# A 4-bit FFN at the end of a decoder: quotients rounded in bf16 from their upper 16 bits, block elements at a pitch, block maxima by halving, and a written order

## The chip, the cores and the metric

The kernel runs on one core of one Trainium2 chip. The metric is device microseconds for one launch. TensorE (PE) does the matmuls and the transposes, VectorE (DVE) most elementwise work and the reductions, ScalarE (ACT) the activation functions and some copies, GpSimd (POOL) a few copies, a cross-partition maximum and some DMA issues; SyncE (SP) only issues DMAs.

## The reference, cut to what matters

A decoder of four layers, each with a self-attention, a cross-attention to a context of 375 rows and an FFN, on x of 8 batches x 112 tokens x 256. Every sublayer is `x = x + f(layernorm(x))`. The change touches the last FFN, whose three matrices and two activations are rounded to a 4-bit format in blocks of 16 consecutive elements:

```python
def fake_quant_nvfp4(x, global_scale):       # blocks of 16 along the last axis
    amax = max(abs(xb))                      # of each block
    sc8  = float8_e4m3fn(clip(amax / 6 * global_scale, 0, 448))
    dq   = sc8 / global_scale
    a    = clip(abs(xb) / dq, 0, 6)
    q    = sign(xb) * nearest of {0, .5, 1, 1.5, 2, 3, 4, 6}
    return q * dq

gate, up = q(x) @ q(gate_w).T, q(x) @ q(up_w).T          # 256 -> 1024
hidden   = silu(gate) * up
out      = q(hidden) @ q(down_w).T                       # 1024 -> 256
```

The weights' global scale is computed from the largest absolute weight of each matrix; the activations' scales are inputs.

## The kernel before

Tokens lie on partitions: 112 of them, one batch at a time, the eight batches side by side. `HB` is 4, half the batches; `HT` is 448, the tokens of a half. The twelve sublayers run one after the other. Within some of them the program's own scheduler orders the instructions of each engine; a `manual_schedule` block instead keeps, on the engines that it names, the order in which the Python code emits them. Each engine executes its list in order, so an instruction that waits holds up all behind it on that engine. Tiles are named by tag; a pool's `bufs` says how many copies of a tag exist, and a new use waits until the readers of the old one are done.

Three places matter here.

**The last FFN, `l3_ffn` (L1940).** It normalises all eight batches (`normalise`: `stats`, then one `tensor_scalar` for each batch, L435), quantises the result in two halves of 112 x 1024 elements, and transposes each half with PE (L1967) into `xqT`. Then, for four pairs of batches: for each batch and each half of the 1024 hidden columns, four matmuls fill the PSUM tile `gu` (two copies), ACT computes `sg`, the silu of the gate (L1983), and DVE the product `hid` (L1984). The pair's 2048 columns are quantised into `hq`, sixteen PE transposes (L1993) and two ACT copies make `hqT` (L1997), sixteen matmuls make the two tiles `y`, and two DVE instructions add them to x (L2001). There is no manual order in this FFN: the scheduler mixes the pairs.

**The helper `quantise` (L1848).** All on DVE. A block's elements are adjacent. It reduces a block to its largest magnitude (L1865), works out the block scale `qs` and the reciprocal `qz` in nine instructions on one element a block (L1867 to L1881), multiplies the source by `qz` (L1884), clamps to +-6 (L1885), isolates the exponent as int32 (L1887), makes from it a rounding constant (L1888), adds and subtracts it (L1889, L1890) and multiplies by the block scale into bf16 (L1891). Everything but the last output is fp32.

**The weights, `l3_weights` (L1893).** Each matrix is 128 x 2048. It is loaded by a POOL DMA into `raw` (one copy, so the next load waits until the last L1884 has read this one), reduced to block maxima `amax` (L1905) and to one column (L1909), POOL takes the maximum across partitions (`gs`, L1910), and two calls of `quantise` follow. This generator is advanced from `l2_ffn`, but the scheduler starts it earlier, between the instructions of the preceding MLP, `mha_mlp` of the second attention of layer 2: there, for each half, PE computes eight `mm` tiles (two copies), ACT takes their gelu `hT` (L1630), and after that PE fills a tile of 112 x 256 for each batch, which DVE adds to `xo` (L1638) and then to x (L1445). The statistics of x follow (L421, L422, then `va` L404 on DVE, the square root `sd` L405 on ACT, which needs a table load of its own, and small DVE steps).

The cross-attention ahead of the FFN (`l3_xattn`, the helper `cross`) has a manual order; the result of batch 3 is added to x (L474) in its middle, that of batch 7 at its end. The first layer's cross-attention `l1_xattn` uses the same helper in the same form.

Of the kernel before, what the change touches and what calls it, by code (L numbers as in the profile page):

```python
# [20 lines left out]
F32 = mybir.dt.float32  # L21
I32 = mybir.dt.int32
BF16 = mybir.dt.bfloat16
AF = mybir.ActivationFunctionType
ALU = mybir.AluOpType
AX = mybir.AxisListType
ET = mybir.EngineType
PSUM = bass.MemoryType.PSUM

P = 128  # L30
S, NB, D = 112, 8, 256
T = S * NB
HT = T // 2
HB = NB // 2
# [9 lines left out]
def _fm(w):  # L44

    k, n = w.shape
    return w.reshape(k // P, P, n).transpose(1, 0, 2).reshape(P, -1)
# [61 lines left out]
def _weights(inp):  # L109
# [3 lines left out]
    a, xa, f = g("L0_attn"), g("L0_xattn"), g("L0_ffn")  # L113
# [33 lines left out]
    a, xa, f = g("L1_attn"), g("L1_xattn"), g("L1_ffn")  # L147
# [23 lines left out]
    for j in range(3):  # L171
        cols = slice(512 * j, 512 * j + 512)
# [10 lines left out]
    a, xa, f = g("L2_attn"), g("L2_xattn"), g("L2_ffn")  # L183
# [44 lines left out]
    a, xa, f = g("L3_attn"), g("L3_xattn"), g("L3_ffn")  # L228
# [13 lines left out]
        ],  # L242
        [("l3x_wo", _fm(_spread(_slots(xa("Wo"))).T))],
    ]
    raw = [_fm(f("gate_w")), _fm(f("up_w")), _fm(f("down_w"))]
    v3 = [
        ("l3f_s_in", np.broadcast_to(f("s_in")[None, :], (P, 1))),
        ("l3f_s_in_down", np.broadcast_to(f("s_in_down")[None, :], (P, 1))),
# [99 lines left out]
class _Kernel:  # L348
# [1496 lines left out]
            )  # L1845
        w.done("l3x_wo")

    def quantise(self, pool, src, dst, rows, n, gs, amax=None):  # L1848


        nc = self.nc
        nb = n // 16

        def blocks(a):
            return a.rearrange("p (k e) -> p k e", e=16)

        def bc(a):
            return a[:, :, None].to_broadcast([rows, nb, 16])

        def sm(tag):  # L1860
            return self.t(pool, [P, nb], f"q{tag}{nb}")[:rows]

        if amax is None:
            amax = sm("m")
            nc.vector.tensor_reduce(amax, blocks(src), AX.X, ALU.max, apply_absolute_value=True)  # L1865
        sc, st, z = sm("s"), sm("t"), sm("z")
        nc.vector.tensor_scalar(sc, amax, 1.0 / 6.0, gs, ALU.mult, ALU.mult)  # L1867
        nc.vector.tensor_scalar(sc, sc, 448.0, None, ALU.min)


        big = 1.5 * 2.0**23
        nc.vector.tensor_scalar(
            st.bitcast(I32), sc.bitcast(I32), 0x7F800000, None, ALU.bitwise_and
        )
        nc.vector.tensor_scalar(st, st, 0.125 * big, 2.0**-9 * big, ALU.mult, ALU.max)
        nc.vector.tensor_tensor(sc, sc, st, ALU.add)
        nc.vector.tensor_tensor(sc, sc, st, ALU.subtract)
        nc.vector.scalar_tensor_tensor(z, sc, 0.0, sc, ALU.is_equal, ALU.add)
        nc.vector.reciprocal(z, z)

        nc.vector.tensor_scalar(z, z, gs, 1.0 + 2.0**-23, ALU.mult, ALU.mult)  # L1881
        a = self.t(pool, [P, n], f"qa{n}")[:rows]
        m = self.t(pool, [P, n], f"qm{n}")[:rows]
        nc.vector.tensor_tensor(blocks(a), blocks(src), bc(z), ALU.mult)  # L1884
        nc.vector.tensor_scalar(a, a, 6.0, -6.0, ALU.min, ALU.max)  # L1885

        nc.vector.tensor_scalar(m.bitcast(I32), a.bitcast(I32), 0x7F800000, None, ALU.bitwise_and)  # L1887
        nc.vector.tensor_scalar(m, m, 1.0, 0.5 * big, ALU.max, ALU.mult)  # L1888
        nc.vector.tensor_tensor(a, a, m, ALU.add)  # L1889
        nc.vector.tensor_tensor(a, a, m, ALU.subtract)  # L1890
        nc.vector.tensor_tensor(blocks(dst), blocks(a), bc(sc), ALU.mult)  # L1891

    def l3_weights(self, pool, ps):  # L1893


        nc = self.nc
        raws, wqs = {}, {}

        def loaded(i):
            raws[i] = self.t(pool, [P, COLS], "raw")  # L1900
            nc.gpsimd.dma_start(raws[i], self.args["in_wq"][i])

        def rounded(i, nk, no):
            amax = self.t(pool, [P, P], "amax")
            nc.vector.tensor_reduce(  # L1905
                amax, raws[i].rearrange("p (k e) -> p k e", e=16), AX.X, ALU.max, apply_absolute_value=True
            )
            top, gs = (self.t(pool, [P, 1], n) for n in ("top", "gs"))
            nc.vector.tensor_reduce(top, amax, AX.X, ALU.max)  # L1909
            nc.gpsimd.partition_all_reduce(gs, top, P, bass_isa.ReduceOp.max)  # L1910
            nc.vector.reciprocal(gs, gs)
            nc.vector.tensor_scalar(gs, gs, 448.0 * 6.0, None, ALU.mult)
            nc.vector.reciprocal(self.igs[:, i : i + 1], gs)
            wqs[i] = self.t(pool, [P, no, nk * P], "wq", BF16)
            flat = wqs[i].rearrange("p o k -> p (o k)")
            for h in range(2):
                cols = slice(h * 1024, (h + 1) * 1024)
                self.quantise(pool, raws[i][:, cols], flat[:, cols], P, 1024, gs, amax[:, h * 64 : (h + 1) * 64])

        def turned(i, nk, no):  # L1920
            out = self.wq[i].rearrange("p (k n) -> p k n", k=nk)
            for k in range(nk):
                tp = self.t(ps, [P, 1024], "tr", BF16)
                for o in range(no):
                    nc.tensor.transpose(tp[:, o * P : (o + 1) * P], wqs[i][:, o, k * P : (k + 1) * P], self.ident16)
                nc.vector.tensor_copy(out[:, k, :], tp[:, : no * P])

        sizes = ((2, 8), (2, 8), (8, 2))
        loaded(0)
        yield  # L1930
        for i in range(4):
            if i > 0:
                turned(i - 1, *sizes[i - 1])
            if i < 3:
                rounded(i, *sizes[i])
            if i < 2:
                loaded(i + 1)
            yield

    def l3_ffn(self):  # L1940
# [3 lines left out]
        with ExitStack() as ctx:  # L1944
# [9 lines left out]
            nc.vector.reciprocal(inv[:, 1:2], s_down)  # L1954
            for i, j in enumerate((0, 0, 1)):
                nc.vector.tensor_tensor(sc[:, i : i + 1], self.igs[:, i : i + 1], inv[:, j : j + 1], ALU.mult)
            self.normalise(self.x, self.xn)
            xq = self.t(acts, [P, NB, D], "xq", BF16)
            xqT = self.t(acts, [P, 2, T], "xqT", BF16)
            for half in range(2):  # L1960
                bs = slice(half * HB, (half + 1) * HB)
                flat = [a[:S, bs, :].rearrange("p b d -> p (b d)") for a in (self.xn, xq)]
                self.quantise(pool, *flat, S, HB * D, s_in[:S])
                tp = self.t(ps, [P, 2, HT], "tr16", BF16)
                for kc in range(2):
                    for j in range(HB):
                        nc.tensor.transpose(  # L1967
                            tp[:, kc, j * S : (j + 1) * S],
                            xq[:S, half * HB + j, kc * P : (kc + 1) * P],
                            self.ident16[:S, :S],  # L1970
                        )
                nc.scalar.copy(xqT[:, :, half * HT : (half + 1) * HT], tp)
            for b0 in range(0, NB, 2):
                hid = self.t(work, [P, 2, 1024], "hid")[:S]
                for j in range(2):
                    xb = self.tokens(b0 + j, xqT)
                    for i in range(2):
                        gu = self.t(ps, [P, 2, 512], "gu")
                        cols = slice(i * 512, (i + 1) * 512)
                        for n, m in enumerate((g, u)):  # L1980
                            self.mm(gu[:S, n, :], [(x, m[:, k, cols]) for k, x in enumerate(xb)])
                        sg = self.t(work, [P, 512], "sg")[:S]
                        nc.scalar.activation(sg, gu[:S, 0, :], AF.Silu, scale=sc[:S, 0:1])  # L1983
                        nc.vector.scalar_tensor_tensor(  # L1984
                            hid[:, j, cols], gu[:S, 1, :], sc[:S, 1:2], sg, ALU.mult, ALU.mult
                        )
                hq = self.t(work, [P, 2, 1024], "hq", BF16)[:S]
                flat = [a.rearrange("p b d -> p (b d)") for a in (hid, hq)]
                self.quantise(pool, *flat, S, 2048, s_down[:S])
                for j in range(2):  # L1990
                    tp = self.t(ps, [P, 8, S], "tr16", BF16)
                    for c in range(8):
                        nc.tensor.transpose(  # L1993
                            tp[:, c, :], hq[:, j, c * P : (c + 1) * P], self.ident16[:S, :S]
                        )
                    hT = self.t(work, [P, 8, S], "hqT", BF16)
                    nc.scalar.copy(hT, tp)  # L1997
                    y = self.t(ps, [P, 512], "y")[:S, :D]
                    self.mm(y, [(hT[:, c, :], d[:, c, :]) for c in range(8)])
                    x = self.x[:S, b0 + j, :]  # L2000
                    nc.vector.scalar_tensor_tensor(x, y, sc[:S, 2:3], x, ALU.mult, ALU.add)  # L2001

    def store(self, out):
        self.nc.sync.dma_start(out.rearrange("b s d -> s b d"), self.x[:S])
# [33 lines left out]
```

## Time and profile before

| | us |
|---|---|
| runs: median (lowest to highest) | 2502.42 (2501.94 to 2503.11) |
| profiled execution | 2510.28 |
| its span | 2508.5 |
| PE busy | 2219.0 (88%) |
| DVE busy | 1464.2 (58%) |
| ACT busy | 795.9 (32%) |
| POOL busy | 212.8 (8%) |

The profile comes from a single execution, 7.9 us longer than the median of the runs. A time such as 2384.51 is in microseconds from the start of the span. The page's busy shares are averages over twelve different sublayers; only a view of the stretch concerned says what holds that stretch up.

### The profile page before, as it was taken

Reading aid. Unit: us, or ns where it says so; the run is one execution under the profiler, and the core shown is the slowest. Engines: PE = TensorE matmul, PEld = TensorE weight load, DVE = VectorE, ACT = ScalarE, POOL = GpSimd, SP = SyncE. Lnnn points to the kernel's source line nnn. Section 1 sums busy time; section 2 is a strip of 40 time slices with the busy share of each in tenths; the row PEclk is TensorE's granted clock in tenths of the full one; section 3 lists DMA queues with packets and bytes.
Section 4 is the critical chain, followed back from the end, with each engine's and each line's share of the span. In section 5 each row is a group of like instructions: output and inputs, shape, how many; then the busy total and the mean of one; then the engine's idle time right before and its main releaser. Section 6 shows DMA issues by size and latency. Waiting matters only on the chain.

```text
span 2508.5 us, 43456 instructions
## 1 busy us (share of the span) xinstructions
PE 2219.0 (88%) x17256; PEld 1347.1 (54%) x17256; DVE 1464.2 (58%) x3879; ACT 795.9 (32%) x1988; POOL 212.8 (8%) x416
## 2 busy tenths in 40 slices
PE   6999999989989889999998887899999999799942
PEld 3444444657655656655666444556555556556622
DVE  4565656555544657763688555767660042667698
ACT  2333333111221245641012222367521111346521
POOL 0111111000001110000111331100000000100000
PEclk9999999786899999999999988899999999799966
DMA  4000001000010000001000001000111000000000
GB/s 182 2 2 2 2 19 61 1 17 1 17 51 1 14 18 2 18 18 42 34 3 35 15 18 59 34 2 1 51 51 50 33 17 1 1 1 2 2 0 15
DMA packets 10730, 56.15 MB, mean 22 GB/s; under 512 B 1833, under 2 KB 3625, under 8 KB 5792
## 3 DMA queue, kind: packets, MB, share of 16 engines
q1 hardware_dynamic: 8304, 44.77, 4.9%
q0 software_dynamic: 2080, 7.07, 0.8%
q8 instruction: 137, 2.24, 0.4%
q10 hardware_dynamic: 144, 1.54, 0.2%
q14 instruction: 65, 0.53, 0.1%
HBM read 52.43 MB, written 0.92 MB: 21 GB/s over the span
## 4 chain that ended last, share of the span: by engine, by line
PE 68%; DVE 21%; issue 5%; ACT 4%; DMA 1%; POOL 1%; DVEq 0%; ACTq 0%; POOLq 0%
PE mm L397 32%; PE tr L1058 6%; PE gu L397 6%; PE g L631 6%; PE sc L397 5%; PE av L1074 3%; PE av L397 3%; DVE rot L1367 1%; ACT sg L642 1%; PE s L397 1%; ACT th L653 1%; DVE hT L657 1%; PE g L609 1%; PE tr L397 1%; DVE h L655 1%
## 5 line engine op out<-in xcount | busy, mean ns | idle before, releaser
L631 PE MATMUL g<-w,hT 128*32 128x256 f32 x3552 | 237.5, 384 | 25.7 <-DVE hT L657 24.4
L397 PE MATMUL mm<-xnT,w 128*128 128x448 f32 x432 | 185.8, 567 | 19.4 <-DVE qT L1370 4.5
L1058 PEld LDWEIGHTS tr<-cst,xe 112*125 112x125 f32 x1152 | 151.3, 188 | 96.2 <-issue 36.9
L1045 DVE TENSOR_REDUCE xnm<-sc 112x1 f32<-112x375 f32 x384 | 184.4, 541 | 28.7 <-PE sc L397 28.0
L1058 PE MATMUL tr<-cst,xe 112*125 112x112 f32 x1152 | 192.7, 289 | 8.6 <-DVE xeT L1066 3.4
L397 PE MATMUL mm<-hT,w 128*128 128x448 f32 x512 | 193.0, 540 | 0.0
L631 PEld LDWEIGHTS g<-w,hT 128*32 128x32 f32 x3552 | 96.0, 109 | 167.0 <-DVE hT L657 124.3
L397 PEld LDWEIGHTS mm<-hT,w 128*128 128x128 f32 x512 | 97.3, 190 | 94.2 <-issue 94.2
L397 PE MATMUL mm<-w,oT 128*112 128x256 f32 x416 | 121.0, 449 | 21.6 <-DVE oT L1547 14.2
L609 PE MATMUL g<-xw,cst 128*32 128x256 f32 x1792 | 138.7, 379 | 0.0
L1066 DVE COPY xeT<-tr 125x336 f32<-125x336 f32 x192 | 97.2, 506 | 69.1 <-PE tr L1058 61.6
L397 PEld LDWEIGHTS mm<-xnT,w 128*128 128x128 f32 x432 | 79.0, 196 | 104.0 <-issue 54.0
L1064 ACT COPY xeT<-tr 125x336 f32<-125x336 f32 x192 | 85.0, 443 | 155.0 <-PE tr L1058 155.0
L397 PE MATMUL mm<-w,hT 128*112 128x256 f32 x576 | 132.3, 389 | 0.2 <-DVE xo L1638 0.2
L1049 ACT ACTIVATE xe<-sc,xnm 112x375 f32<-112x375 f32 x256 | 126.3, 582 | 9.2 <-DVE xnm L1045 9.2
L397 PE MATMUL gu<-xnT,w 128*128 128x448 f32 x320 | 124.4, 544 | 1.7 <-DVE hT L1212 1.2
L397 PEld LDWEIGHTS mm<-w,hT 128*112 128x112 f32 x576 | 103.5, 182 | 27.5 <-issue 4.9
L397 PEld LDWEIGHTS mm<-w,oT 128*112 128x112 f32 x416 | 83.9, 211 | 53.4 <-DVE oT L1547 14.4
L642 ACT ACTIVATE sg<-g 128x192 f32<-128x192 f32 x224 | 73.9, 330 | 105.3 <-PE g L631 93.9
L653 ACT ACTIVATE th<-cell 128x64 f32<-128x64 f32 x224 | 57.4, 256 | 146.8 <-DVE cell L651 146.7
L474 DVE TENSOR_TENSOR x<-mm,x 112x256 f32<-112x256 f32 x64 | 27.0, 422 | 129.8 <-PE mm L397 129.8
L655 DVE TENSOR_TENSOR h<-sg,th 128x64 f32<-128x64 f32 x224 | 50.5, 225 | 84.5 <-ACT th L653 84.5
(381 smaller groups left out, 3755.8 us busy)
## 6 DMA issues: line engine op xcount, KB each, us to landing
w<-in_w SPq DMA_DIRECT2D x33, 1024.0 KB, 4.9
w<-in_w SPq DMA_DIRECT2D x4, 896.0 KB, 11.4
raw<-in_wq POOLq DMA_DIRECT2D x3, 1024.0 KB, 5.1
wi<-in_wint POOLq DMA_DIRECT2D x3, 768.0 KB, 6.0
w<-in_w SPq DMA_DIRECT2D x2, 768.0 KB, 4.2
ctxT<-in_ctxT ACTq DMA_DIRECT2D x1, 1500.0 KB, 8.4
cx<-in_ctx POOLq DMA_DIRECT2D x1, 1500.0 KB, 21.0
w<-in_w SPq DMA_DIRECT2D x2, 512.0 KB, 4.0
```

The source lines that it names most:

```text
L397: self.nc.tensor.matmul(out, lhsT, rhs, start=i == 0, stop=i == len(pairs) - 1)
L609: nc.tensor.matmul(g[32 * j : 32 * j + 32, :], pick[:, t % 16, :], xw[:, l, t // 16, 256 * j : 256 * j + 256], start=True, stop=t == 0, sk ...
L631: nc.tensor.matmul(g[32 * j : 32 * j + 32, :], hT[l][:, c, :], whh[l][:, c, 256 * j : 256 * j + 256], start=False, stop=c == 1, skip_group ...
L642: nc.scalar.activation(sg[:, :192], g[:, :192], AF.Sigmoid)
L653: nc.scalar.activation(th, cell[l], AF.Tanh)
L655: nc.vector.tensor_tensor(h, og, th, ALU.mult)
L1045: nc.vector.tensor_reduce(nm, sc, AX.X, ALU.max, negate=True)
L1049: nc.scalar.activation(e, sc, AF.Exp, bias=nm)
L1058: nc.tensor.transpose(tp[:CH, i * S : (i + 1) * S], e[:, i * CH : (i + 1) * CH], self.ident[:S, :S])
L1064: nc.scalar.copy(eT, src)
L1066: nc.vector.tensor_copy(eT, src)
L1074: nc.tensor.matmul(avs[b][32 * j : 32 * j + 32, c * S : (c + 1) * S], values[b % 2][:CH, i, 4 * c + j, :], eTs[b, c, j][:, i, :], start=i ...
```

## The change

The columns of the weights are permuted on the host, so that within a row of `row` elements a block's 16 elements lie at a pitch of `row`/16: `row` is 256 for x and for the gate and up matrices, 1024 for the hidden activations and the down matrix. The normalisation writes its output into that order. In `quantise`:

- the block maximum of an activation comes from |source| (`mag`, an absolute value on ACT) by four `tensor_tensor` maxima, each of half the length of the one ahead of it; the weights keep one `tensor_reduce`, now over a strided view;
- the quotient is still an fp32 product; its upper 16 bits, with the lowest bit set, become a bf16 number; clamp, exponent, constant, addition and subtraction work on bf16;
- the block scale is kept in bf16, and the last product is taken in parts of 1024.

`quantise` becomes a generator. In `l3_ffn` each half of the batches has statistics of its own, and the pairs run under a `manual_schedule`: the next pair's hidden activations between the steps of this pair's quantisation, this pair's two results after the two parts of its last product, and its additions to x within the next pair's quantisation. The diff, cut to its core:

```diff
-    raw = [_fm(f("gate_w")), _fm(f("up_w")), _fm(f("down_w"))]
+    of = [np.arange(n).reshape(-1, 16).T.ravel() for n in (D, 1024)]
+    raw = [_fm(f("gate_w")[of[1]][:, of[0]]), _fm(f("up_w")[of[1]][:, of[0]]), _fm(f("down_w")[:, of[1]])]
...
+    def block_max(self, pool, src, rows, n, row):
+        nb, k = n // 16, row // 16
+        e, a = 16, src.rearrange("p (r e k) -> p r e k", e=16, k=k)
+        while e > 1:
+            e //= 2
+            out = self.t(pool, [P, nb * e], f"qm{nb * e}")[:rows]
+            o = out.rearrange("p (r e k) -> p r e k", e=e, k=k)
+            self.nc.vector.tensor_tensor(o, a[:, :, :e, :], a[:, :, e : 2 * e, :], ALU.max)
+            a = o
+        return out
...
-            nc.vector.tensor_reduce(amax, blocks(src), AX.X, ALU.max, apply_absolute_value=True)
+            amax = self.block_max(pool, mag, rows, n, row)
+            yield
...
-        nc.vector.tensor_tensor(sc, sc, st, ALU.subtract)
-        nc.vector.scalar_tensor_tensor(z, sc, 0.0, sc, ALU.is_equal, ALU.add)
+        nc.vector.tensor_tensor(s16, sc, st, ALU.subtract)
+        nc.vector.scalar_tensor_tensor(z, s16, 0.0, s16, ALU.is_equal, ALU.add)
...
-        nc.vector.tensor_tensor(blocks(a), blocks(src), bc(z), ALU.mult)
-        nc.vector.tensor_scalar(a, a, 6.0, -6.0, ALU.min, ALU.max)
-        nc.vector.tensor_scalar(m.bitcast(I32), a.bitcast(I32), 0x7F800000, None, ALU.bitwise_and)
-        nc.vector.tensor_scalar(m, m, 1.0, 0.5 * big, ALU.max, ALU.mult)
-        nc.vector.tensor_tensor(a, a, m, ALU.add)
-        nc.vector.tensor_tensor(a, a, m, ALU.subtract)
-        nc.vector.tensor_tensor(blocks(dst), blocks(a), bc(sc), ALU.mult)
+        b, m = (self.t(pool, [P, n], f"q{i}{n}", BF16)[:rows] for i in "bp")
+        nc.vector.tensor_tensor(wide(a), wide(src), bc(z), ALU.mult)
+        yield
+        high = a.bitcast(I16).rearrange("p (n two) -> p n two", two=2)[:, :, 1]
+        nc.vector.tensor_scalar(b.bitcast(I16), high, 1, None, ALU.bitwise_or)
+        yield
+        nc.vector.tensor_scalar(b, b, 6.0, -6.0, ALU.min, ALU.max)
+        nc.vector.tensor_scalar(m.bitcast(I16), b.bitcast(I16), 0x7F80, None, ALU.bitwise_and)
+        nc.vector.tensor_scalar(m, m, 1.0, 96.0, ALU.max, ALU.mult)
+        yield
+        nc.vector.tensor_tensor(b, b, m, ALU.add)
+        nc.vector.tensor_tensor(b, b, m, ALU.subtract)
+        yield
+        for at in range(0, n, 1024):
+            part = slice(at, at + 1024)
+            half = s16[:, at // 16 : at // 16 + 64].rearrange("p (r k) -> p r k", k=k)
+            nc.vector.tensor_tensor(
+                wide(dst[:, part]), wide(b[:, part]),
+                half[:, :, None, :].to_broadcast([rows, 64 // k, 16, k]), ALU.mult,
+            )
+            yield
...
-                amax, raws[i].rearrange("p (k e) -> p k e", e=16), AX.X, ALU.max, apply_absolute_value=True
+                amax.rearrange("p (r k) -> p r k", k=nk * 8),
+                raws[i].rearrange("p (r e k) -> p r k e", e=16, k=nk * 8),
+                AX.X, ALU.max, apply_absolute_value=True,
...
-            self.normalise(self.x, self.xn)
...
+                mv, rs = self.stats(self.x[:, bs, :], S, HB)
+                for j in range(HB):
+                    nc.vector.tensor_scalar(
+                        self.xn[:S, b0 + j, :].rearrange("p (e k) -> p k e", e=16),
+                        self.x[:S, b0 + j, :].rearrange("p (k e) -> p k e", e=16),
+                        mv[:S, j, 0:1], rs[:, j : j + 1], ALU.subtract, ALU.mult,
+                    )
...
+                        nc.scalar.activation(mags[b0][:, j, cols], hids[b0][:, j, cols], AF.Abs)
+                        yield
...
+            def result(b, hq):
+                tp = self.t(ps, [P, 8, S], "tr16", BF16)
+                for c in range(8):
+                    nc.tensor.transpose(tp[:, c, :], hq[:, c * P : (c + 1) * P], self.ident16[:S, :S])
+                hT = self.t(work, [P, 8, S], "hqT", BF16)
+                nc.scalar.copy(hT, tp)
+                ys[b] = self.t(ps, [P, 512], "y")[:S, :D]
+                self.mm(ys[b], [(hT[:, c, :], d[:, c, :]) for c in range(8)])
...
+            with tc.manual_schedule(engines={ET.PE, ET.DVE, ET.Activation}):
+                for _ in hidden(0):
+                    pass
+                for b0 in range(0, NB, 2):
...
+                    for step, _ in enumerate(self.quantise(pool, *flat, S, 2048, 1024, s_down[:S], mag=mag)):
+                        if step == 1 and b0 > 0:
+                            add(b0 - 2)
+                            add(b0 - 1)
+                        if step >= 2:
+                            next(later, None)
+                        if step >= 6:
+                            result(b0 + step - 6, hq[:, step - 6, :])
+                add(NB - 2)
+                add(NB - 1)
```

## The prediction

> **What bounds the kernel now.** The page comes first: PE has 88% of the span and the chain of work that ended last is 68% PE, but the last slices show DVE at 6 to 9 tenths, so the end has another limit. The table by stretches settles it. Its columns are stretch and length, then busy us (and instructions) of PE, PE weight loads, DVE, ACT and POOL, then the granted clock, DMA share and GB/s:
>
> ```profile
> 2350.00:2375.00 25.00, 22.30 (x245) 15.95 (x244) 16.74 (x36) 14.23 (x32) 0.61 (x1) 1.00 0.01 2
> 2375.00:2400.00 25.00, 6.87 (x47) 4.40 (x45) 16.59 (x44) 2.02 (x3) 0.61 (x1) 0.63 0.00 1
> 2400.00:2425.00 25.00, 14.57 (x56) 7.59 (x57) 24.23 (x38) 9.84 (x13) 0.00 (x0) 0.70 0.00 0
> 2425.00:2450.00 25.00, 10.67 (x49) 6.82 (x49) 24.65 (x27) 4.46 (x6) 0.00 (x0) 0.70 0.00 0
> ```
>
> Up to 2375 (the last cross-attention) PE is full; from 2400 DVE is, with 24.2 to 24.7 us of 25. So a microsecond saved on DVE in the FFN is a microsecond. The FFN stretch runs from the last statistics (2385.61) to the last addition to x (2502.62): 117.0 us. The groups of that stretch (line, operation, tiles, shapes, busy, mean ns, idle before) give the prices:
>
> ```profile
> L1884 DVE TENSOR_TENSOR qa<-hid,qz 112x2048 f32<-112x2048 f32 x4 | 9.2, 2293 | 0.1
> L1865 DVE TENSOR_REDUCE qm<-hid 112x128 f32<-112x2048 f32 x4 | 9.1, 2278 | 0.0
> L1885 DVE TENSOR_SCALAR qa<-qa 112x2048 f32<-112x2048 f32 x4 | 4.9, 1224 | 0.1
> L1984 DVE SCALAR_TENSOR_TENSOR hid<-gu,sc,sg 112x512 f32<-112x512 f32 x16 | 11.9, 745 | 0.1
> ```
>
> Idle before each is 0.1 us in all: nothing else holds DVE up. Two other places are touched: the middle of the last cross-attention, and the weights' rounding inside the MLP of layer 2. There the timeline (start, length, engine, line) reads:
>
> ```profile
> 1819.62 0.42 DVE L1638 TENSOR_TENSOR xo<-mm,xo 112x256 f32<-112x256 f32 x1
> ...
> 1834.59 0.16 DVE L404 TENSOR_SCALAR va<-mv 112x4 f32<-112x4 f32 x1
> 1834.85 2.29 DVE L1905 TENSOR_REDUCE amax<-raw 128x128 f32<-128x2048 f32 x1
> ```
> ```profile
> 1820.09 7.16 PE L397 MATMUL mm<-w,hT 128*112 128x256 f32 x32 [0.17 <-DVE xo L1638]
> ...
> 1836.99 4.78 PE L397 MATMUL mm<-xnT,w 128*128 128x448 f32 x12 [0.93 <-ACT hT L1630]
> ```
>
> PE is the bound, has no slack to DVE (it waits 0.17 us for the first addition to xo), and waits 0.93 us for a gelu that is queued on ACT behind the square root, which waits for va on DVE.
>
> **What the Trainium skill says.** "VectorE: DVE Perf Modes" (the perf-mode tier table): for 2048 elements fp32 tensor_tensor 2293 ns, fp32 tensor_scalar 1227; the trace agrees (2293, 1224). For bf16 it gives 1224 and 693 ns; no row here shows that. "Vector Engine (DVE) Microarchitecture Reference", section 5.1: the 16-bit pairing needs a step of one on every tensor, and a row read again and again still pairs. So clamp, exponent and constant get the 693, sums and last product the 1224, but the OR, whose source steps over every other half-word, stays at the fp32 rate. Section 5.2 of the same page: single words far apart stream at 1.7 to 2.5 ns an element instead of 1.05. The trace agrees faintly, on eight-element operations: a read at a pitch of eight words takes 172 ns, its neighbour with adjacent words 166 in the median. "ScalarE: Activation LUTs" (What ACT_TABLE_LOAD costs): 1283 ns a load; the trace has 1.28.
>
> **The change part by part.**
>
> *DVE work of a pair (2048 elements).* Before: reduction 2.28, nine small ones 3.06, four tensor_tensor at 2.29 (9.16), three tensor_scalar at 1.22 (3.67): 18.2. After: maxima of 1024, 512, 256, 128 outputs, at the tensor_tensor slope 1.22 + 0.69 + 0.42 + 0.29 = 2.62; small ones 3.06; product 2.29; OR 1.22; three at 0.69 = 2.07; two sums 2.44; last product 2 x 0.69 = 1.38: 15.1. Saved 3.1, four times: 12.4. *A half of x (1024)*, in the same way: 10.5 before, 1.62 + 2.32 + 1.23 + 0.69 + 1.27 + 1.38 + 0.69 = 9.2 after; saved 1.3, twice: 2.6. The halves' separate statistics move four normalisations (L435, 0.33 each as they follow one another) out of this stretch: 1.3 more. Together 16.3. Halving itself costs 0.35 a pair; what it buys is only that the sign is dropped on ACT.
>
> *The written order gives part back.* I played the order of the changed kernel through with these durations, 0.035 us between dependent DVE instructions and 0.07 between engines. (1) The first pair's hidden activations: ACT's list is silu, absolute value, silu, absolute value, each waiting for the last DVE product, so a piece costs silu 0.69 + product 0.74 + about 0.62, and DVE idles some 3.6 us, where the scheduler had filled in other pairs' work. (2) In the loop the second product finds its silu 0.3 us late behind the OR, three times: 0.9. (3) The additions of a pair stand after the next block scales, 6.1 us after the last product. PE is by then at: transposes 0.93, copy 0.91, eight y matmuls 1.9 (before, the first eight take that), then transposes, copy and matmuls of the second batch: 6.9 to 7.8 us. DVE waits up to 1 us, three times: 1.5. (4) At the end the second batch's transposes stand behind the first's matmuls: 6.9 to 7.9 us from the last product to the end, against 5.4 before (2497.25 to 2502.62): +2.0. Sum 8.0, so the stretch shrinks by 16.3 - 8.0 = **8.3**; played through it ends at 105.7 with PE's second matmuls fast and 109.9 with them slow. I take **8.5 less** (108.5).
>
> *Statistics of half 0 in the last cross-attention.* Two table loads and a square root enter ACT's list between exponentials, small DVE steps and four normalisations DVE's. The first layer has this very event (timeline, the additions of batches 2 to 5):
>
> ```profile
> 994.26 0.42 DVE L474 TENSOR_TENSOR x<-mm,x 112x256 f32<-112x256 f32 x1 [0.35 <-PE mm L397]
> 1013.76 0.43 DVE L474 TENSOR_TENSOR x<-mm,x 112x256 f32<-112x256 f32 x1 [0.35 <-PE mm L397]
> 1034.57 0.42 DVE L474 TENSOR_TENSOR x<-mm,x 112x256 f32<-112x256 f32 x1 [0.34 <-PE mm L397]
> 1054.06 0.42 DVE L474 TENSOR_TENSOR x<-mm,x 112x256 f32<-112x256 f32 x1 [0.34 <-PE mm L397]
> ```
>
> A period is 19.5 us, the one with the statistics 20.8: **+1.3**. The normalisation now writes at a pitch of 16 words; at worst that doubles its 0.33 us, so bounds 1.3 to 2.6, taken **+1.7**.
>
> *The weights.* Each matrix saves about 3.4 us of DVE, and the third runs under matmuls that never wait for DVE: worth nothing. But the reduction L1905 now reads single words 16 (third matrix 64) apart. Unknown, from 2.28 us (no penalty) to 5.3 (2.5 ns each); from the 172 against 166 ns, 0.8 ns more an element, 3.9, so +1.6. Two consequences. First, L1909, POOL's maximum and gs (1813.27) come 1.6 later, and with them the first addition to xo, which the shorter rounding brings forward by only 0.3: PE waits 1.2 more. Second, in the new DVE order the second matrix's reduction stands ahead of the last statistics and va; it was behind. va comes near 1837.6, though the data lands 3.8 us earlier, since raw is read sooner and POOL's next DMA issue waits for that alone. Behind va wait the square root, a table load and the gelus, and with them PE: 3.5 us instead of 0.93: +2.5. Sum **+3.7**, 0.4 at the lower bound and 6.5 at the upper. No SP issue is moved.
>
> *Sum:* -8.5 + 1.7 + 3.7 = -3.1; the profiled execution would go from 2510.3 to 2507.2. It was 7.9 slower than the median of the runs, so I subtract from that: 2502.4 - 3.1 = 2499.3, rounded to 2499.
>
> **The rivals.** *(A) Strided access is free.* For it: runs of two words at a larger pitch show no penalty in this trace; against it, the 172 ns. Then 8.5 - 1.3 - 0.4 = 6.8 is left: 2495.6. With PE fast in the y matmuls as well, 9.6: 2493. *(B) Slower, by the strided reduction.* At 2.5 ns an element MLP and cross-attention cost 6.5 + 2.3, and the gain is gone. It turns into a clear loss if the three bf16 tensor_scalar fall to the fp32 rate too: played through, +6.3 on the FFN. Together -8.5 + 6.3 + 8.8 = +6.6: 2509. The single mechanism decides from about 5.2 us a reduction. *(C) The OR at one element a cycle*, 2.29: +4.1 played through, ending 1 us slower than before, 2503.4. Against it: fp32 and int32 tensor_scalar run at two a cycle here.
>
> **How the numbers follow.** About 0.2% (5 us) is what a measurement of this kernel can tell from no change. The forecast, with its own range 2496.5 to 2502.5, gets 0.46; A 0.35, since it needs only small errors in my give-backs besides; C 0.07; B 0.12. A lies mostly past 5 us faster, and a part of the forecast does: faster 0.44, within 0.2% 0.47, slower 0.09. The range, 2493 to 2505, leaves out most of B and the far end of A.
>
> **What would show it.** Right: bf16 tensor_scalar of 2048 near 0.69 us and the OR near 1.22; the FFN stretch near 108; one period of the last cross-attention near 21 us; PE waiting over 3 us for a gelu near 1835; the strided reduction near 3.9. The prediction is wrong if that reduction stays at 2.28 (A), if it nears 5.3 or bf16 brings no rate (B), or if DVE waits over 12 us in the loop.

## The result and the profile after

The changed kernel takes **2496.75 us** in the median (14 runs, 2492.67 to 2499.96); the kernel before, on the same chip, takes 2501.89 (14 runs, 2498.75 to 2503.11). The ratio is 0.9978, with a 95% interval of 0.997 to 0.9986: 5.1 us faster, between 3.5 and 7.5. Predicted were 2499.0 and a range of 2493 to 2505.

The two profiled executions are further apart than the medians: spans of 2508.5 and 2495.2. The stages tell why. Each row below is a difference of two start times in the timeline; the marks are the first va of the MLP of layer 2, the transposes that end that MLP, the first and the last addition of the last cross-attention, and the end of the last addition to x.

| Stretch | before | after | difference | predicted |
|---|---|---|---|---|
| start to va (code that is the same) | 1800.12 | 1794.36 | -5.8 | 0 |
| MLP of layer 2, va to transposes | 54.68 | 56.51 | +1.8 | +3.7 |
| from there to the last cross-attention (layer-2 FFN, layer-3 attention) | 404.15 | 402.97 | -1.2 | 0 |
| last cross-attention, first to last addition | 125.56 | 126.46 | +0.9 | +1.7 |
| last addition there to the end | 118.11 | 109.00 | -9.1 | -8.5 |

The first row is no gain of the change. In the fourteen profiles of this study va starts between 1793.2 and 1802.6, and the third stretch takes 400.1 to 404.2, though what stands in front of it is the same. The last two rows repeat. The cross-attention takes 125.56 in the three profiles with all statistics at the end, and 126.15 to 126.46 in the eleven others; the last row comes to 118.11 and 118.18 in two profiles with the old code, to 109.00 and 108.87 in two with the new, and to between 99.0 and 99.2 in the four below that have the scheduler's order there with bf16. The MLP as changed takes 56.2 to 56.6 in five profiles, but 58.5 in a sixth, in which PE's matmuls after its wait ran at a lower clock (last section). Summed over the places that the change touches, the profile says -6.4; the medians say -5.1, with -7.5 to -3.5 as their interval. From here on, stages are compared, not spans.

**The stretches** of the end, the last two windows of the prediction's (columns: PE, PE weight loads, DVE, ACT, POOL, clock, DMA share, GB/s):

```profile
2400.00:2425.00 25.00, 9.79 (x32) 4.62 (x31) 20.70 (x31) 9.62 (x16) 0.00 (x0) 0.70 0.00 0
2425.00:2450.00 25.00, 13.95 (x72) 10.29 (x72) 23.33 (x42) 8.59 (x13) 0.00 (x0) 0.64 0.00 1
```

From 2400 on DVE had 24.2 and 24.7 of 25 us; now it has 20.7 and 23.3. It is still the fullest engine, but it has begun to wait. Over the whole stretch from the last statistics to the end, one line of the same view holds the balance for each kernel, before first:

```profile
2385.61:2502.62 117.01, 42.95 (x208) 28.39 (x208) 109.27 (x141) 21.02 (x28) 0.00 (x0) 0.65 0.00 0
```
```profile
2381.40:2489.30 107.90, 46.72 (x208) 31.00 (x208) 92.19 (x165) 32.41 (x47) 0.00 (x0) 0.62 0.00 0
```

DVE works 17.1 us less (109.27 to 92.19), though it has 24 instructions more. It is idle for 15.7 us instead of 7.7. So 8.0 us of the saving went into new waits.

**The groups** (busy, mean ns of one, idle before) give the rates that were unknown:

```profile
L1907 DVE TENSOR_SCALAR qb<-qa 112x2048 int16<-112x2048 int16 x4 | 4.9, 1221 | 0.0
...
L1914 DVE TENSOR_TENSOR qb<-qb,qp 112x2048 bf16<-112x2048 bf16 x4 | 4.9, 1218 | 0.0
...
L1909 DVE TENSOR_SCALAR qb<-qb 112x2048 bf16<-112x2048 bf16 x4 | 2.7, 686 | 0.0
```

The OR over every other half-word runs at 1.22 us for 2048 elements, the clamp in bf16 at 0.69, a sum at 1.22.

**DVE's waits** in that stretch (us in total, times, longest):

```profile
DVE x L2052 <- PE y L400: 8.6, 5, 3.4
DVE hid L2035 <- ACT sg L2034: 2.9, 2, 2.2
DVE qm L1859 <- ACT mag L2038: 0.7, 1, 0.7
```

The lower two are the first pair's chain of silu, product and absolute value: 3.6 us. The first is three waits of 0.64 in the loop, and the end, where PE's timeline shows why it is long:

```profile
2481.10 0.93 PE L2044 MATMUL tr<-ident,hq 112*128 112x112 bf16 x8 [9.47 <-DVE hq L1920]
2483.08 1.96 PE L400 MATMUL y<-wq,hqT 128*112 128x256 bf16 x8 [1.05 <-ACT hqT L2046]
2484.83 0.95 PE L2044 MATMUL tr<-ident,hq 112*128 112x112 bf16 x8
2486.83 1.96 PE L400 MATMUL y<-wq,hqT 128*112 128x256 bf16 x8 [1.05 <-ACT hqT L2046]
```

Transposes, copy, matmuls, and then all three once more: the second batch's transposes stand behind the first one's matmuls, and each copy on ACT is waited for (1.05).

**The last cross-attention**, its additions to x:

```profile
2312.31 0.42 DVE L477 TENSOR_TENSOR x<-mm,x 112x256 f32<-112x256 f32 x1 [0.35 <-PE mm L400]
2333.13 0.42 DVE L477 TENSOR_TENSOR x<-mm,x 112x256 f32<-112x256 f32 x1 [0.34 <-PE mm L400]
2352.62 0.42 DVE L477 TENSOR_TENSOR x<-mm,x 112x256 f32<-112x256 f32 x1 [0.35 <-PE mm L400]
```

From the first to the second is a period of 20.82, from there to the third one of 19.49 like the others: +1.33, as in the first layer. The last interval before the end is half a microsecond shorter (8.52 instead of 9.02), so the stage grows by only 0.9.

**The MLP of layer 2**, DVE's reduction and va, then PE:

```profile
1825.34 3.59 DVE L1938 TENSOR_REDUCE amax<-raw 128x128 f32<-128x2048 f32 x1
...
1829.58 0.17 DVE L407 TENSOR_SCALAR va<-mv 112x4 f32<-112x4 f32 x1
...
1831.98 6.28 PE L400 MATMUL mm<-xnT,w 128*128 128x448 f32 x16 [3.18 <-ACT hT L1633]
```

The strided reduction takes 3.6 us instead of 2.28, stands ahead of va, and PE waits 3.18 us for a gelu instead of 0.93.

### The profile page after: what moved, and what is told of

Same layout as the page of the kernel before. It is cut to its first block, busy times and chain, and to the rows that moved or that the text cites. A ratio compares the mean times of both kernels' runs of the same rounds, so it can differ in the third digit from the quotient of the medians.

```text
span 2495.2 us, 43496 instructions
## 1 busy us (share of the span) xinstructions
PE 2215.5 (89%) x17256; PEld 1342.1 (54%) x17256; DVE 1440.5 (58%) x3919; ACT 809.6 (32%) x2009; POOL 212.9 (9%) x416
## 4 chain that ended last, share of the span: by engine, by line
PE 69%; DVE 19%; issue 5%; ACT 4%; DMA 1%; POOL 1%; DVEq 0%; ACTq 0%; POOLq 0%
PE mm L400 33%; PE tr L1061 6%; PE gu L400 6%; PE g L634 6%; PE sc L400 5%; PE av L1077 3%; PE av L400 3%; DVE rot L1370 1%; ACT sg L645 1%; PE s L400 1%; ACT th L656 1%; DVE hT L660 1%; DVE cell L654 1%; DVE h L658 1%; PE tr L400 1%
## 5 line engine op out<-in xcount | busy, mean ns | idle before, releaser
L1061 PEld LDWEIGHTS tr<-cst,xe 112*125 112x125 f32 x1152 | 151.3, 187 | 97.6 <-issue 36.7
```

The costliest lines, as they stand in the source:

```text
L1061: nc.tensor.transpose(tp[:CH, i * S : (i + 1) * S], e[:, i * CH : (i + 1) * CH], self.ident[:S, :S])
```

## The experiments

The diffs are shortened to their sense. Ratios are to runs of the kernel before on the same chip, with 95% intervals; a figure for a stage comes from one profile. The changed kernel's own is 0.9978, and 0.001 is 2.5 us. "End" is the last row of the table above: from the start of the last addition of the cross-attention to the end of the last addition to x.

### The order of the results

```diff
-    tr(b0); copy; y(b0)          # at step 6
-    tr(b0 + 1); copy; y(b0 + 1)  # at step 7
+    tr(b0); copy                 # at step 6
+    tr(b0 + 1); copy; y(b0); y(b0 + 1)
```

> Edit to the changed kernel: in the last FFN both batches of a pair are transposed and copied before either down matmul. Theory (the order of the results costs time): in the changed kernel the end runs transposes 0.93, copy 0.91, matmuls 1.95, then the same three again, 7.66 us from the last product to the end, and each pair's additions wait 0.64 us for the second batch's matmuls. With both transposes ahead a copy, and the first batch's matmuls, no longer stand in the way: tail 5.7 us (-2.0), the three waits of 0.64 gone (-1.9). FFN stretch 107.9 to 104.0; time 2496.8 to 2493. Rival (the waits only move): the two copies stand together on ACT ahead of the next silu or PE is the limit anyway; only the tail is shortened: stretch 106, time 2495.

Measured: ratio 0.9959 (0.9947 to 0.9972); end 103.8, that is **-5.2**, more than either theory said. PE's last lines:

```profile
2483.21 1.67 PE L2046 MATMUL tr<-ident,hq 112*128 112x112 bf16 x16 [10.73 <-DVE hq L1920]
2485.19 2.68 PE L400 MATMUL y<-wq,hqT 128*112 128x256 bf16 x16 [0.30 <-ACT hqT L2048]
```

The three waits of 0.64 are gone (-1.9), and the copies no longer stand between. DVE's waits for y fall from 8.6 to 3.7 us. The theory holds. That it was too small is partly chance: the last sixteen matmuls took 2.68 us in one go, where two separate eights took 1.96 each, but the sixteens of the three earlier pairs took 3.66, 3.12 and 3.66 in this same profile. The MLP, which this edit leaves alone, took 58.5 here.

### The statistics of half 0

```diff
-for half in range(2): mv, rs = stats(x[half]); normalise 4 batches
+mv, rs = stats(x); normalise 8 batches   # once, after the last addition
```

> Edit to the changed kernel: statistics and normalisations of all 8 batches once, after the last addition, as in the kernel before; all else as changed. Theory (the statistics of half 0 cost 1.3 us where they were put, but hide more than that at the end): the long period of the last cross-attention goes from 20.8 back to 19.5 us (-1.3); the FFN stretch gains four normalisations (4 x 0.34) and, since half 0's maxima no longer fill the wait for the square root, about 1.5 more: 107.9 to 110.8; time 2496.8 to 2498.3. Rival (the move is worth its price only): FFN stretch 109.2, time unchanged within 0.3.

Measured: ratio 0.998 (0.997 to 0.999); the long period is gone (19.50, all alike) and the last interval is back at 9.02, so the cross-attention is 0.9 shorter, 125.56 as before; end 111.4, **+2.4**. The move costs 0.9 and brings 2.4: a net gain of 1.5 us, too small for the timing to show. The theory holds.

### The written order taken away

```diff
-with tc.manual_schedule(engines={ET.PE, ET.DVE, ET.Activation}):
+if True:   # the scheduler orders the same instructions
```

> Edit to the changed kernel: the written order of the last FFN's main loop is taken away; the scheduler orders the same instructions. Theory (the written order gives back about 8 of the 16 us that the arithmetic saves; of these the first pair's 3.6, the late additions 1.9 and part of the tail are the order's): in the scheduler's order products of other pairs fill the first pair's waits: FFN stretch 107.9 to 102.5, time near 2491. Rival (the order is as good as any, what is given back lies in the dependencies): the scheduler's order leaves as many waits elsewhere, stretch 107 to 110, time 2496 to 2499.

Measured: 2488.96 against 2503.34 before, ratio **0.9939** (0.9926 to 0.9953); end 99.0, **-10.0**: twice what the theory gave. Its stretch line:

```profile
2381.71:2479.61 97.90, 41.48 (x208) 29.14 (x208) 88.62 (x164) 32.10 (x47) 0.00 (x0) 0.67 0.00 0
```

DVE's waits for other engines fall from 12.2 to 7.3 us (-4.9), which is what was expected. But the busy time falls too, by 3.6 us, with the same instructions. A piece of DVE's timeline shows the other half:

```profile
2413.11 0.29 DVE L1897 TENSOR_TENSOR qh<-qs,qt 112x128 bf16<-112x128 f32 x1
2413.43 0.29 DVE L1898 SCALAR_TENSOR_TENSOR qz<-qh 112x128 f32<-112x128 bf16 x1
2413.64 1.22 DVE L1859 TENSOR_TENSOR qm<-mag 112x1024 f32<-112x1024 f32 x1
2414.78 0.94 DVE L1899 RECIPROCAL qz<-qz 112x128 f32<-112x128 f32 x1
```

The second line depends on the first and starts 0.03 us after its end. The third belongs to the next pair and starts 0.08 before its predecessor ends; so does the fourth. Alternating two pairs' instructions saves about 0.11 us at each step: busy time is counted once where two overlap, and the small gaps go as well (the rest, -1.5). The instructions themselves got no shorter: their durations, overlaps counted twice, add up to 97.6 us in the written order and to 97.0 in the scheduler's. The written order runs each pair's nine small operations one behind the other.

### What the reduction's stride costs

```diff
-raw "p (r e k) -> p r k e"   # 16 words at a pitch
+raw "p (k e) -> p k e"       # 16 adjacent words
```

> Edit to the changed kernel: the weights' maxima are taken over 16 adjacent words instead of 16 words at a pitch (maxima of other blocks, so other scales; the rest is as changed). Theory (in the MLP the second reduction, 3.6 us, stands ahead of va, and PE waits for that): the reduction takes 2.28 us, va comes 1.3 us earlier, PE waits 1.9 instead of 3.18 for the gelu, the MLP and the time are 1.3 us shorter: 2495.5. Rival (the wait is set by the table loads or the data's landing): the reduction shortens, PE's wait stays near 3.2, time unchanged.

Measured: ratio 0.9972 (0.9961 to 0.9982). Both reductions take 2.27 to 2.29; PE waits 2.14; the MLP takes 55.56, **-0.95**. The second reduction now waits 0.23 for its data, hence less than 1.3. The theory holds for these 1.0 us of the wait; 2.14 are left, against 0.93 in the kernel before. The time alone could not have shown it.

### The first pair between the steps of half 1

```diff
-for _ in hidden(0): pass            # after both halves of x
+for step, _ in enumerate(half_1):   # pieces of pair 0 from the second step on
+    if step >= 1: next(first, None)
```

> Edit to the changed kernel: the first pair's hidden pieces are written between the steps of the rounding of half 1 of x (they need only half 0), instead of after it. Theory (DVE's 3.6 us of waits there are the chain silu, product, absolute value of a pair that has no other work beside it): the waits for a silu and for the absolute value go from 3.6 to under 1; from the last addition of the cross-attention to the end 109.0 to 106; time 2496.8 to 2494. Rival (ACT or PE is the limit there, the chain only starts earlier): the waits move into the rounding of half 1, 109.0 to 108.5, time unchanged.

Measured: ratio 0.9962 (0.9947 to 0.9977); end 106.4, **-2.6**. In the table of waits the silus' fall from 2.9 to 1.0 us, that for the absolute value is gone, and those for y stay at 8.6.

The theory holds: the chain was long because it had no other work beside it.

### The rounding in fp32

```diff
-b = bf16 tile; b = high half of a | 1; clamp, exponent, sums in bf16
+b = a; clamp, exponent, sums in fp32      # order: the scheduler's
```

> Edit to the changed kernel with its written order taken away (the run with the scheduler's order is its base): quotients, exponents and sums stay in fp32, without the OR; pitch, halving and statistics as changed. Theory (all of the saving is bf16's rates; pitch and halving bring none by themselves): per pair three tensor_scalar 0.69 to 1.22, two sums 1.22 to 2.29, last product 1.37 to 2.29, minus the OR 1.22: +3.4, four times, and +1.7 for each half: +17.2. From the last addition of the cross-attention to the end 99.0 (base) to 116; time 2489 to 2506. Rival (pitch and halving carry part of it, bf16 is worth the 10 us that the order gives back): 109 and 2499.

Measured: 2505.72 against 2504.9 before, ratio 1.0 (0.9992 to 1.0008); end 115.7, **+16.7** on its base of 99.0 (predicted 17.2). The saving goes with bf16: without it the pitch, the halving and the split statistics together bring the end from 118.1 only to 115.7, and the split alone brought 2.4 in the written order. The reverse, bf16 without the pitch, was not run, so how much of bf16's rates depends on the pitch stays open.

### A plain reduction for the maxima

```diff
-mag = Abs(hid) on ACT; maxima of 8, 4, 2, 1 rows
+tensor_reduce(amax, hid "p (r e k) -> p r k e", max, abs)
```

> Edit to the changed kernel, in its written order: in the last FFN the block maxima are one reduction with absolute value over the pitched blocks, as for the weights, instead of halving; ACT's absolute values are left out with it. Theory (halving is cheaper than a strided reduction, and costs the first pair its place on ACT): reduction 3.6 against 2.62 plus gaps for 2048, 4 x 0.9, and about 0.3 for each half: +4.2; ACT's 0.63 drop out of the first pair's chain and the wait of 0.69 for the last goes: -2.5. Together +1.7: time 2498.5. Rival (112-partition activations stream the pitch faster, at 2.28): -3.5: 2493. A reduction at over 4 us: 2501.

Measured: end 106.0, **-3.0**, with a reduction of 3.6 us:

```profile
L1885 DVE TENSOR_REDUCE qm<-hid 112x128 f32<-112x2048 f32 x4 | 14.4, 3604 | 0.0
```

Ratio 0.9972 (0.996 to 0.9983), too close to 0.9978 to tell. This theory fell, and the rival's reason was wrong as well. DVE is busy 3.5 us more (95.65), as the price of the reduction says, but its waits shrink from 12.2 to 6.7: the first pair's are gone altogether, not 2.5 of 3.6, since the silus now run ahead of the products; and in the loop the longer reduction gives PE the time that it needed, so the additions wait 1.9 less. There are fewer instructions and fewer gaps (-1.0). Dropping the sign on ACT made halving possible, and in the written order cost more than halving saved; in the scheduler's order this was not run.

### All three, and va ahead of the reduction

```diff
-raw loaded by POOL's queue; written order; tr, y, tr, y
+raw loaded by SP's queue; scheduler's order; tr, tr, y, y
```

> Three edits to the changed kernel together: the scheduler's order in the last FFN, both transposes of a pair ahead of its down matmuls, and the weights' matrices loaded by SP's queue instead of POOL's, which in the order as built puts va ahead of the second matrix's reduction. Theory (a reduction of 3.6 us ahead of va is the MLP's loss): PE's wait for the gelu goes from 2.9 to 3.4 to under 0.5, from the first reduction to the transposes after the MLP 52.8 to 49.8 (-3); tail one us shorter than in the scheduler's order alone: 2489 to 2485. Rival (SP's wait for the raw buffer delays the weights behind it, or the data lands late): the MLP stays at 52 or longer: 2488 to 2490.

Measured: ratio 0.9942 (0.993 to 0.9954), no better than the scheduler's order alone; end 99.1. The MLP is longer, 57.6 (55.2 by the mark of the forecast, where 49.8 had been expected). Two things had been overlooked. In the new order the first matrix's reduction stands ahead of the normalisation of xn, for which PE then waited up to 1.30 us. And in the scheduler's order PE's sixteen transposes already stood ahead of its matmuls, so there was nothing to gain at the end. The part about va did come true in half: with va ahead of the second reduction, and the square root still behind two gelus, PE waited 1.16 for the gelu instead of 2.87.

```profile
1835.29 6.28 PE L400 MATMUL mm<-xnT,w 128*128 128x448 f32 x16 [1.16 <-ACT hT L1633]
```

```diff
 # base: the scheduler's order in the last FFN
+tensor_tensor(last, raw[:, :1], wq[:, -1:], max)   # holds raw until its rounding ends
```

> Two edits to the changed kernel: the scheduler's order in the last FFN (as in the run with that alone, its base), and one small operation that reads the first raw matrix at the end of its rounding, so that the second matrix is loaded some 5 us later and its reduction stands behind va in DVE's order; nothing else moves in the order there. Theory (in the MLP the second reduction ahead of va is the whole loss): PE's wait of 2.9 for the gelu goes under 0.3; from the first va of the MLP to the transposes behind it 56.2 (base), 54.7 (kernel before) to 53.3; time 2489 to 2486. Rival (va is held by the last addition to xo, or the later load delays the second rounding into the hidden matmuls): wait still over 1.5, 55.5 or more, time unchanged.

Measured: 2489.49 against 2505.08, ratio **0.9934** (0.9921 to 0.9948); end 99.1. va came 3.2 us earlier (31.7 after the first va, not 34.9), and **the theory still fell**: PE waited 2.00, and the MLP took 57.0, 0.8 more than its base. The rival's figures came true, but not by its reasons. ACT's timeline tells it, first of the kernel before, then of this one:

```profile
1828.79 0.63 ACT L1630 ACTIVATE hT<-mm,vec 128x448 f32<-128x448 f32 x1 [15.10 <-PE mm L397]
1830.29 0.64 ACT L1630 ACTIVATE hT<-mm,vec 128x448 f32<-128x448 f32 x1 [0.87 <-PE mm L397]
1831.80 0.63 ACT L1630 ACTIVATE hT<-mm,vec 128x448 f32<-128x448 f32 x1 [0.87 <-PE mm L397]
1832.45 1.28 ACT L405 ACT_TABLE_LOAD   x1
1834.79 0.20 ACT L405 ACTIVATE sd<-va 112x4 f32<-112x4 f32 x1 [1.06 <-DVE va L404]
```
```profile
1826.28 0.63 ACT L1633 ACTIVATE hT<-mm,vec 128x448 f32<-128x448 f32 x1 [14.68 <-PE mm L400]
1826.93 1.28 ACT L408 ACT_TABLE_LOAD   x1
1829.91 0.21 ACT L408 ACTIVATE sd<-va 112x4 f32<-112x4 f32 x1 [1.70 <-DVE va L407]
```

The square root stood after three gelus of the second half before the change, after two with it, and after one here; the gelus behind it wait. It seems that the scheduler puts it where it expects va, but what it reckons with was not looked at: from the kernel before to the changed one the square root moved forward, although va came later (8.68 us after PE began the second half, not 7.51).

For PE both count, the place and the time of va. Behind two gelus, va came 8.68, 7.64 and 6.23 us after PE began the second half (changed kernel, adjacent words, all three edits), and PE waited 3.18, 2.14 and 1.16. At another place the same va costs something else: behind three gelus, in the kernel before, 7.51 cost 0.93; behind four, in the run with fp32 rounding, 11.17 cost 2.22; behind one, here, 5.13 cost 2.00.

Here the clock then cost nearly as much as the wait did: PE's next twenty matmuls took 9.48 us, where sixteen took 6.28 in the changed kernel. The second line is a stretch of 5 us, columns as above, with a granted clock of 0.66:

```profile
1832.11 9.48 PE L400 MATMUL mm<-xnT,w 128*128 128x448 f32 x20 [2.00 <-ACT hT L1633]
```
```profile
1833.00:1838.00 5.00, 5.00 (x10) 2.39 (x9) 3.32 (x1) 1.27 (x2) 0.00 (x0) 0.66 0.19 79
```

### The square root left out

```diff
-sd = sqrt(va) on ACT; rs = 1 / sd
+rs = 1 / va      # half 0 ahead of the layer-2 FFN only
```

> Edits to the changed kernel with the scheduler's order in the last FFN (the run with that alone is the base): the statistics of half 0 ahead of the layer-2 FFN, which lie inside the MLP, leave out the square root (the reciprocal of the variance is used in its place, so the values differ); the second reduction stays ahead of va. Theory (what reaches PE is only ACT's list: the square root stands after two gelus of the second half, earlier than in the kernel before, and the gelus behind it wait for va): without it PE's wait of 2.9 is gone, from the first va of the MLP to the transposes behind it 56.2 to 53.3. Rival (DVE's late normalisation of x, or the additions to xo behind the reduction, hold PE too): over 55.

> The same edit to the kernel before. Theory: its wait of 0.93 is gone, 54.7 to 53.7; if the changed kernel's run comes to the same 53.5 within 0.3, the whole loss of the change in the MLP (1.8) went through that wait, and the longer strided reduction costs nothing by itself there. Rival: the two differ by over 1 us: part of the loss is elsewhere.

Measured: 53.07 us in the changed kernel (with the scheduler's order), 53.12 in the kernel before; ratios 0.9925 (0.9901 to 0.9949) and 0.9997 (0.9983 to 1.001). PE of the former no longer waits:

```profile
1826.31 12.19 PE L400 MATMUL mm<-xnT,w 128*128 128x448 f32 x32
1838.34 13.98 PE L400 MATMUL mm<-w,hT 128*112 128x256 f32 x64
```

The theory holds: the two kernels differ by 0.05 us, so the MLP's whole loss of 1.8 went through that one square root in ACT's list (with it go its two table loads and four small steps of DVE). Without it the reduction of 3.6 us, the shorter rounding and va's place cost PE nothing. In the kernel before, too, the MLP fell by more than its wait of 0.93: by 1.6.

### The written order mended

Three of the edits above together: first pair early, transposes first, va ahead; the written order is kept.

> Three edits to the changed kernel, written order kept: first pair's pieces between the steps of half 1, both transposes of a pair ahead of its down matmuls, va ahead of the second reduction. Theory (the edits add up, since each takes away another wait): from the last addition of the cross-attention to the end 109.0 - 2.6 - 5.2 = 101.2; MLP 56.5 to 53.3; together -11: 2486. It stays 2 us behind the scheduler's order in that stretch (99.0), because in a row of dependent small operations DVE starts each after the one before, whereas alternating ones overlap by 0.08. Rival (with the first pair done early, ACT's copies and silus collide): 104 and 2489.

Measured: 2492.2 against 2505.08, ratio 0.9944 (0.9931 to 0.9956); end 102.1, MLP 57.1. At the end the edits add up to -6.9 of the -7.8 expected. What is missing is about what the last sixteen matmuls took longer: 3.66 us here, 2.68 where the transposes alone were put first. To the scheduler's order 3 us remain: DVE is busy 91.78, not 88.6. The MLP brought nothing, as with va ahead in the scheduler's order: the square root stands after one gelu, PE waited 2.03, and the clock was 0.66 over the next 5 us.

Of the versions that leave nothing out, the fastest is the changed kernel with the scheduler's order in the last FFN: 0.9939, with va ahead 0.9934, with all three edits 0.9942. The three can't be told apart.

## Why the prediction was right, step by step

**DVE's work and what the order gives back.** Predicted were 16.3 us saved and 8.0 given back; measured 17.1 and 8.0. The bf16 rates are those that the Trainium skill gives ("VectorE: DVE Perf Modes", perf-mode tier table): 693 and 1224 ns there, 686 and 1218 here. The OR stayed at the fp32 rate as argued. The give-backs one by one: the first pair 3.6 for 3.6; the products behind the OR 0.4 for 0.9; the additions 1.9 for 1.5; the end 7.66, inside 6.9 to 7.9. The y matmuls ran slow in each of these places, the end of the range that I had left open. The stretch shrank by 9.1, predicted 8.5. That this is so close is in part luck. Of the give-backs one was 0.5 too large and two together 0.7 too small. And with slow matmuls the play-through had given a stretch of 109.9, 2.0 more than the 107.9 measured; taking 108.5, between its two ends, hid that.

**Cross-attention**, predicted +1.7, measured +0.9. The event taken from the first layer was exact (+1.33). Two terms were mis-sized: the normalisation that writes at a pitch costs next to nothing (0.33 to 0.35 from start to start, about 0.33 without the pitch), and the last interval became 0.5 shorter, which I had not looked for. The run with late statistics shows that this belongs to the move, since it was 9.02 again there. The time is PE's: the last batch's four transposes (L1104) take 0.60 us instead of 1.01, with a granted clock of 1.00 in the two us around them; it is 0.55 before and 0.58 with late statistics. What raised it was not followed.

**The weights**, predicted +3.7, measured +1.8: here a step failed. The reduction was sized well, 3.6 for 3.9: 1.76 ns an element, within the 1.7 to 2.5 of "Vector Engine (DVE) Microarchitecture Reference", section 5.2. PE's wait was 3.18 for 3.5. What failed is the step by which POOL's maximum and gs come 1.6 later and PE waits 1.2 more. gs came 13.15 us after the first va before, 13.11 after the change, and 13.23 with the reduction at 2.27: the reduction does not set it. The idle time ahead of POOL's maximum (PARTITION_ALL_REDUCE) said so, had I followed it:

```profile
1812.86 0.38 POOL L1910 PARTITION_ALL_REDUCE gs<-top  x1 [7.82 <-issue]
```

Its releaser is its own issue: it starts 7.8 us after POOL's previous operation in both kernels, 5.4 and 4.0 us after the DVE result is there. In the run with SP's queue POOL's previous operation ended 4.5 us later after va, and gs came 4.7 later. The Trainium skill has a place for it ("GPSIMD Engine Reference", section 2.1): the first call of a freshly loaded routine pays some 6 us that no instruction in the profile shows; the 7.8 us here could be of that kind, but that they are a load was not tried. So the strided reduction hides there, the shorter rounding brings the first addition forward, and PE's 0.17 us of wait vanish. The second step, +2.5 by forecast and +2.25 in PE's wait, was right in size and half right in its cause. I had the later va as the only reason, and va did come 1.2 us later, counted from PE's start on the second half (8.68, not 7.51). The other 1.1 are the place of the square root in ACT's list, one gelu further forward, which I had not considered.

**The rivals.** (A), free strided access, was wrong about the read and right about the write. Its time of 2495.6 was nearer than the forecast's, for another reason: the gs step cost nothing, and the cross-attention less than taken. (B) needed 5.3 us a reduction, (C) an OR of 2.29: neither happened. Nor did DVE wait over 12 us in the loop; it waited 1.9 there.

**The median.** I subtracted 3.1 from it; the touched stages say 6.4, the medians 5.1. Taking the sum from the median and not from the profiled time was right: in the code that the change leaves alone the two profiled executions differ by 7.0 us (first and third row of the table), which is most of the 7.9 by which the one of the kernel before lies above its median.

## What to carry to other kernels

When arithmetic on the bounding engine gets shorter, add up its busy and its idle time over the stretch for both kernels: the difference in idle time is what new waits take back, and here it was half of the gain. An order written by hand should alternate independent chains on an in-order engine, and keep a second engine's helper work out of the chain that feeds the first. An operation that waits on an in-order engine is charged to those queued behind it: before moving its input, look at what place it has in that engine's list, and at how late its input comes there.

## What had not been expected of the hardware

- On DVE an instruction that doesn't depend on the one before starts 0.08 us before that one ends; one that does starts 0.03 after. Alternating two chains instead of running one behind the other took away 3.6 us of busy time and 1.5 us of gaps, in a stretch that then took 98 us.
- Sixteen bf16 matmuls of 256 columns in one go took from 2.68 to 3.66 us, within one run too; eight after a pause of 1.05 us took 1.96. The Trainium skill's "TensorE: Matmul & The Clock Gate" (Part 1) says that the clock follows PE's load over a window that runs free of the program. That fits what the waits of the MLP show: over the 5 us that followed the wait, the clock was 0.66 after 2.00, 2.03 and 3.36 us of waiting, but 1.00 after 2.14, 2.87, 2.96 and 3.18. The length of a wait in this range does not tell whether the clock falls. Where it fell, the MLP lost some 2 us more than the wait itself, against the 53.1 us of the runs without the square root; where it did not, 0.3.
- A one-source reduction that reads single words at a pitch costs 1.76 ns an element, with 112 partitions as with 128. A normalisation that writes at a pitch of 16 words starts as often as without it (every 0.33 to 0.35 us), though its own record grows from 0.41 to 0.50 us.
